# Two chained cross-attention layers on one core: an attention transfer issued in the first step, ScalarE's half of some norms a step later, output weights' sums in step 24, one copy of e by VectorE, the last pair in two stores

## The chip, the cores and the metric

The kernel runs on one core of one Trainium2 chip. The core has TensorE (PE in the profile, its weight loads PEld), VectorE (DVE), ScalarE (ACT), GpSimd (POOL) and SyncE (SP), and 16 DMA engines that the queues of SP, ScalarE and GpSimd feed. The metric is the device time of one execution in microseconds: the median over several executions. All data is float32.

## The reference

Inputs are `x` and a context, both [32, 256, 256]: 32 batches of 256 tokens of width 256. The first layer is an attention with 16 heads between `x` and the context, of which only batch 0 is used and added to every batch. The second layer is, for every batch, a cross-attention from the sum (normalised) to the context (normalised), a hidden layer of width 4 with GELU, a self-attention on its normalised output, and two skip connections.

```python
att = attention(tgt @ Wq.T, memory @ Wk.T, memory @ Wv.T)   # 16 heads of 16
x = tgt + att[0]                                            # batch 0's, added to all 32

norm_X   = layernorm(ctx, norm1_w, norm1_b)
norm_F_L = layernorm(x, norm2_w, norm2_b)
attended = softmax(norm_F_L @ norm_X.T / 16) @ norm_X
h = gelu(attended @ fc1_w.T + fc1_b)                        # width 4
cross = h @ fc2_w.T + fc2_b
norm_cross = layernorm(cross, norm3_w, norm3_b)
self_att = softmax(norm_cross @ norm_cross.T / 16) @ norm_cross
out = norm_F_L + gamma2 * (cross + gamma1 * self_att)
```

## The kernel before

A batch's 256 tokens lie two to a partition, so one batch of x is a [128, 2, 256] piece of the tile `x_all` (batch n, an even and an odd half), and likewise for the context in the tiles `cq` (four batches to a tile, four tiles). Everything stays in SBUF; each batch is loaded once and stored once.

**Stage 1 (to about 34 us)** is the first layer on batch 0. Its result is the tile `att`. From there on `att` has to be added to all 32 batches. Batches 0 to 3 are added by VectorE (`add_first`, and line 844 for batch 2). The others are added by transfers that `add_attention(lo, hi)` (L750) issues on GpSimd's queue, four batches and 1 MB to a transfer, with the DMA engines adding to what `x_all` holds.

**Stage 2** is `first_step(s)` (L869), called for s = 0 to 31 and, for what trails behind, 32 to 34. Step s does the scores and the exponentials of batch s. Around them it works ahead and behind: it turns e of batch s-2 (`cross_turned`), takes the statistics (VectorE) of x and of the context of batches some steps ahead, forms their means and factors (`moments_...`, on GpSimd, with one slow power instruction, L227), normalises (`norm_x`, `norm_c`), turns x of batch s+1 (`turn_x`) and the context of batch s+4 (`turn_c`). For a batch of x, `norm_x` (L326) gives the even half to GpSimd (L329) and the odd half to ScalarE (L331); ScalarE's instruction stands in that engine's queue between the copies of the turned x of the same step (L761, into `nfT`) and the exponentials (L792). Every four steps a group of four batches goes through `values`, `cross_values` and `cross_weighted`, and the lists `between` (inside the step, ahead of its scores) and `beside` (behind the step) add the work of the hidden layer and the first scores of the self-attention (`early_scores`, `early_weights`), step by step. The self-attention is done on vectors of 5 or 6 numbers, with small Gram products on GpSimd (`times_gram`, L1010).

The engines run their instructions in the order in which this code emits them, each engine its own queue; semaphores hold an instruction until what it needs is there. PSUM has two banks each for the tags `tp` (turned x, context, and smaller pieces), `et` (turned e), and `sm` and `s` in stage 2, so a transpose also waits until the copy out of the bank it is given is done.

`output_gammas`, `output_bias` and `output_rows` (L645 to L658) form the rows of the output weights on VectorE, six instructions on 5 partitions, and copy them with eight small transfers on SP's queue into `w_out`, which the last stage multiplies with.

**Stage 3 (from about 175 us)** is the rest of the self-attention and the output, in an order written out by hand as a string of words (L1244); `o12@s1` is the output product of pair 12 (batches 24 and 25), `add12` the sum of it with `x_all` on VectorE (`output`, L1211), followed by the pair's store on SP's queue. The stores are 512 KB each, 16 in all.

```python
        if s in (2, QB):
            add_attention((s // 2 + 2) * QB, (s // 2 + 3) * QB)
        elif b == 0 and 1 < q < NQ - 3:
            add_attention((q + 3) * QB, (q + 4) * QB)

        late_turn = s in (27, 29, 31)
        if 0 <= s - 2 < B and not late_turn:
            cross_turned(s - 2)
```

(QB is 4, B is 32; q and b are s // 4 and s % 4.)

Of the kernel before, what the change touches and what calls it, by code (L numbers as in the profile page):

```python
# [22 lines left out]
QB = 4  # L23
# [4 lines left out]
def tile_xattn_seq(  # L28
# [33 lines left out]
    nc = tc.nc  # L62
    B = x.shape[0]
# [16 lines left out]
    def bank(tag, name):  # L80
        return ps.tile([P, NC, D], F32, tag=tag, name=name)


    x_all = const.tile([P, B, NC, D], F32)
# [3 lines left out]
    def by_tokens(src):  # L88
        return src.rearrange("b (p t) d -> p b t d", t=NC)

    def load_c(q, first=0, queue=nc.sync):
        if q not in cq_of:
            cq_of[q] = ld.tile([P, QB, NC, D], F32, tag="cq", name=f"cq_{q}")
        n = 1 if first else QB
        lo = q * QB + (1 if first == 2 else 0)
        hi = q * QB + (1 if first == 1 else QB)
        queue.dma_start(cq_of[q][:, lo - q * QB : hi - q * QB], by_tokens(mem[lo:hi]))

    def load_x(lo, hi):
        nc.sync.dma_start(x_all[:, lo:hi], by_tokens(x[lo:hi]))  # L100
# [96 lines left out]
    def turned(src, tag, name, psum=None):  # L197

        pt = psum(f"pt_{name}") if psum else bank(tag, f"pt_{name}")
        for dc in range(NC):  # L200
            for t in range(NC):
                nc.tensor.transpose(  # L202
                    pt[:, dc, t * P : (t + 1) * P], src[:, t, dc * P : (dc + 1) * P], ident
                )
        return pt
# [39 lines left out]
    st_of, mc_of, mx_of = {}, {}, {}  # L245
# [7 lines left out]
    def stats_c(n):  # L253
        q, b = n // QB, n % QB
        statistics(st_tile(q - 1)[:, 0, b], cq_of[q][:, b])

    def stats_x(n):
        q, b = n // QB, n % QB
        statistics(st_tile(q)[:, 1, b], x_all[:, n])
# [16 lines left out]
    def moments_x(q, lo, hi):  # L276
        rn = moments(flat(st_of[q][:, 1, lo:hi]), (hi - lo) * NC, f"x{q}_{lo}")
        for b in range(lo, hi):
            mx_of[q * QB + b] = *rn, (b - lo) * NC
# [44 lines left out]
            )  # L324

    def norm_x(n, even=nc.gpsimd):  # L326
        rs, nmr, i = mx_of.pop(n)
        row = x_all[:, n, 0, :]
        even.tensor_scalar(row, row, rs[:, i, :], nmr[:, i, :], ALU.mult, ALU.add)  # L329
        row = x_all[:, n, 1, :]  # L330
        nc.scalar.activation(  # L331
            row, row, AF.Identity, bias=nmr[:, i + 1, :], scale=rs[:, i + 1, :]
        )


    nxT_of, nfT_of, col_of, eT_of, e_of = {}, {}, {}, {}, {}
# [324 lines left out]
    on_scalar = nc.scalar.copy  # L661

    by_vector = nc.vector.tensor_copy
# [86 lines left out]
    def add_attention(lo, hi):  # L750
        nc.gpsimd.dma_start(
            x_all[:, lo:hi],
            att.unsqueeze(1).to_broadcast([P, hi - lo, NC, D]),
            accum_op=ALU.add,
        )
# [38 lines left out]

        return softmax

    def cross_turned(n):
        q, b = n // QB, n % QB
        if b == 0:
            eT_of[q] = wk.tile([P, QB, NC, D], F32, tag="eTq", name=f"eTq_{q}", bufs=2)  # L800
        nc.scalar.copy(eT_of[q][:, b], turned(e_of.pop(n), "et", f"e_{n}"))  # L801

    def values(q):

# [22 lines left out]
    def add_first(n):  # L827
        nc.vector.tensor_add(x_all[:, n], x_all[:, n], att)
        stats_x(n)
# [39 lines left out]
    def first_step(s, between=()):  # L869
        q, b = s // QB, s % QB  # L870
        if b == 0 and 2 <= q and q + 4 < NQ:
            load_c(q + 4)
            if q == 2:
                load_x((NQ - 2) * QB, B)
        if s in (2, QB):
            add_attention((s // 2 + 2) * QB, (s // 2 + 3) * QB)
        elif b == 0 and 1 < q < NQ - 3:
            add_attention((q + 3) * QB, (q + 4) * QB)

# [3 lines that stand above are left out]
        if 2 <= s < 2 * QB:  # L883
            for n in (2 * s, 2 * s + 1):
                stats_x(n)
            if s < QB:
                ends = first_moments(2 * s, 2 * s + 2)
        if QB <= s and s + 3 * QB < B:
            stats_c(s + 3 * QB)
        if s >= 2 * QB and s + 2 * QB < B:  # L890
            stats_x(s + 2 * QB)
        if b == QB - 1 and 4 <= q + 2 < NQ:
            if q + 3 < NQ:
                moments_both(q + 2)
            else:
                moments_x(q + 2, 0, QB)
        if QB < s < B - 1:
            turn_x(s + 1)
        for n in {9: (12,), 10: (13, 14), 11: (15,)}.get(s, ()):
            norm_x(n)  # L900
        if 3 * QB <= s < B - 2 * QB:
            norm_x(s + QB)
        elif B - 2 * QB < s <= B - QB:
            norm_x(s + QB - 1)
        if s + QB < B and s >= QB:
            turn_c(s + QB, on_scalar if s < QB + 2 else by_vector)
        for n in {7: (13,), 8: (14, 15), 9: (16, 17), 10: (18,)}.get(s, ()):
            norm_c(n)
        if 2 * QB + 2 < s < B - 2 * QB:
            norm_c(s + 2 * QB)  # L910
        for n, at in enumerate(scaled_at):
            if s == at:
                scale_skip(n)
        if 2 * QB <= s < 2 * QB + len(zeroed):
            nc.gpsimd.memset(*zeroed[s - 2 * QB])
        if b == 2 and 1 < q < NQ:
            values_turned(q)
        if b == 1 and 1 < q < NQ:
            values(q)
        if b == 2 and 0 < q <= NQ:  # L920
            cross_values(q - 1)
        if b == 3 and 0 < q <= NQ:
            cross_weighted(q - 1)
        for f, *args in between:
            f(*args)
        if s < B:
            softmax = cross_scores(s)
            if s <= QB:
                turn_x(s + 1)
            if s == 0:  # L930
                turn_c(6, nc.scalar.copy)
            softmax()
        if late_turn:
            cross_turned(s - 2)
        if 1 <= s <= QB:
            stats_c(s + 3 * QB - 1)
        if s == 0:
            first_ends.pop()()
            add_first(3)
            first_ends.append(first_moments(3, QB))  # L940
            odd_normed(7)
        elif s == 1:
            first_ends.pop()()
            odd_normed(8)
            even_normed(8, 9)
        elif s == 2:
            ends()
            turn_c(7)
            load_c(5)
            odd_normed(9)  # L950
            even_normed(10)
        elif s == 3:
            ends()
            values(1)
            even_normed(11)
        elif s == QB:
            values_turned(1)
        if s in (QB, QB + 1):
            odd_normed(s + 6)
        if s == QB:  # L960
            moments_x(2, 0, 2)
        elif s == QB + 1:
            norm_x(2 * QB)
            moments_x(2, 2, QB)
        elif s == QB + 2:
            norm_x(2 * QB + 1)
            moments_c(3)
            norm_x(2 * QB + 2)
            norm_c(3 * QB)
        elif s == QB + 3:  # L970
            norm_x(2 * QB + 3)
        elif s == 2 * QB:
            moments_both(3)
# [146 lines left out]
    def divide(g, pa):  # L1120
        rd = small.tile([P, TQ, 1], F32, tag="rd2", name=f"rd2_{g}")
        nc.vector.reciprocal(rd, pa[:, :, NM : NM + 1])
        nc.vector.tensor_mul(
            v_flat[:, g * TQ : (g + 1) * TQ, NM : 2 * NM],
            pa[:, :, 0:NM],
            rd.to_broadcast([P, TQ, NM]),
        )
# [25 lines left out]
    def activate(lo):  # L1153
# [1 line left out]

    between = {
        20: [(hide, 0, 4)],
        24: [(output_gammas,)],
        25: [(output_bias,)],
        27: [(output_rows,)],  # L1160
        28: [(turn_t, 0, by_vector)],
        29: [(turn_u, 2, by_vector), (early_weights, 0), (hide, 4, 6)],
        30: [(activate, 4), (third_a, 2), (turn_t, 1, by_vector)],
# [3 lines left out]
        20: [(activate, 0), (third_a, 0)],  # L1167
        21: [(third_b, 0), (third_a, 1)],
        22: [(third_c, 0), (third_b, 1)],
        24: [(third_d, 0)],  # L1170
        25: [(third_c, 1), (turn_u, 0, by_vector)],
        26: [(turn_u, 1, by_vector), (early_scores, 0), (third_d, 1)],
        28: [(early_scores, 1)],
# [37 lines left out]
    def output(p, pieces):  # L1211
        for lo, hi, po in pieces:
            xs = x_all[:, 2 * p + lo : 2 * p + hi]
            nc.vector.tensor_add(xs, po, xs)  # L1214
        nc.sync.dma_start(by_tokens(out[2 * p : 2 * p + 2]), x_all[:, 2 * p : 2 * p + 2])


    held = {}

# [35 lines left out]
    turn_t6 add8 scale27 sums7 tT6 add7 turn_v5 col7 scale28 o9@s1+k12@s0 vT5 k13@et  # L1255
    add9 exp12 scale29 turn_a7 exp13 o10@s0+o11@s1 scale30 a7 sums6 add10 scale31
    turn_v7 col6 add11 vT7 turn_a6 o15@s0+o14@et a6 turn_v6 add15 vT6 o12@s1 add14
    o13@s0 add12 add13
    """

    def turn_a(g):
# [15 lines left out]
    def pre(lo):  # L1277
# [9 lines left out]
        "max": lambda p: scores_max(p, held.pop(("q", p))),  # L1287
        "exp": lambda p: weights(p, held.pop(("k", p))),
        "add": lambda p: output(p, held.pop(("o", p))),
        "a": lambda g: divide(g, held.pop(("a", g))),  # L1290
        "sums": sums,
        "col": col,
# [69 lines left out]
```

## Time and profile before

| | |
|---|---|
| time, median of 3 | 227.26 us (227.24 to 228.19) |
| the profiled execution's own time | 228.16 us |
| its span in the profile | 226.4 us |
| TensorE, VectorE, ScalarE, GpSimd busy | 208.1, 169.8, 146.6, 175.3 us |
| bytes moved by DMA | 33.81 MB |
| ScalarE's waits for GpSimd's factors at L331 | 11.0 us in 4 waits |
| last sum of VectorE done | 221.42 us |

The span runs from the first to the last instruction of the program; the time has some 2 us around it. In the profile a row of the timeline has its start in us from the span's start, its length in us, the engine, the line of the kernel, the operation, the tiles written and read with buffer numbers left out, the shape, and in brackets for how long the engine stood idle before it and what ended that. A row of the chain has start, length, engine and line: it is the way back from the last instruction, each time to what released it. Since an engine's queue is strictly in order, an instruction that waits holds all those behind it on that engine.

### The profile page before, as it was taken

How to read it: one execution, taken by the hardware profiler on the slowest of the kernel's cores; microseconds unless marked ns; L12 is line 12 of the kernel's file. 1: busy time of each engine (PE TensorE's matmuls, PEld its weight loads, DVE VectorE, ACT ScalarE, POOL GpSimd, SP SyncE). 2: the span in 40 equal slices, each digit the busy share in tenths (PEclk: the TensorE clock that was granted, in tenths of full speed). 3: DMA queues.
4: the chain of work that ended last, by engine and by line, in shares of the span. 5: the costliest groups of instructions: out<-in, count | busy, mean ns of one | idle time of the engine just before them, and what ended most of it. 6: DMA issues, size and time to landing. Idle time of an engine off the chain costs nothing.

```text
span 226.4 us, 4951 instructions
## 1 busy us (share of the span) xinstructions
PE 208.1 (92%) x1797; PEld 152.6 (67%) x1797; DVE 169.8 (75%) x406; ACT 146.6 (65%) x301; POOL 175.3 (77%) x276
## 2 busy tenths in 40 slices
PE   7899988898999989999999999998998999999960
PEld 6666547576787859688798697685756566666640
DVE  2787989898988766768767578596546699978791
ACT  2454877698979359576868986448594684545510
POOL 6056588567889999999979989999229888999700
PEclk9999999999999999999999999999999999999996
DMA  6699998998976994082280000000000031542786
GB/s 210 214 310 375 389 386 225 179 263 246 208 145 244 305 195 185 0 147 43 48 142 0 1 3 0 0 3 5 5 1 0 3 126 62 210 164 92 278 308 254
DMA packets 18038, 33.81 MB, mean 149 GB/s; under 512 B 1175, under 2 KB 2142, under 8 KB 18014
## 3 DMA queue, kind: packets, MB, share of 16 engines
q1 hardware_dynamic: 12974, 24.33, 30.1%
q0 software_dynamic: 3696, 7.34, 18.6%
q10 hardware_dynamic: 1344, 1.84, 2.5%
q8 instruction: 14, 0.23, 0.4%
q14 instruction: 10, 0.08, 0.1%
HBM read 17.73 MB, written 8.39 MB: 115 GB/s over the span
## 4 chain that ended last, share of the span: by engine, by line
PE 45%; POOL 22%; DVE 14%; DMA 8%; ACT 5%; issue 3%; DVEq 1%; ACTq 0%; SPq 0%; POOLq 0%
PE sc L779 8%; POOL cq L307 6%; PE o L445 4%; DMA x_all<-att 4%; POOL rs_b L227 4%; PE k L445 4%; DVE st L211 4%; PE pu L357 4%; POOL x_all L329 3%; PE sc L445 2%; PE q L445 2%; DVE nm L789 2%; DMA wk_nat<-in_L_xattn_Wk_dram 2%; DMA fc_nat<-in_L_xattn_fc_w_dram 2%; POOL rs_x L227 2%
## 5 line engine op out<-in xcount | busy, mean ns | idle before, releaser
L779 PE MATMUL sc<-nxT,nfT 128*128 128x256 f32 x256 | 62.4, 386 | 0.7 <-ACT nfT L761 0.7
L779 PEld LDWEIGHTS sc<-nxT,nfT 128*128 128x128 f32 x256 | 45.7, 190 | 12.1 <-issue 5.3
L770 POOL TENSOR_TENSOR x_all<-x_all,w_bc 128x512 f32<-128x512 f32 x32 | 39.8, 1278 | 0.0
L792 ACT ACTIVATE e<-sc,nm 128x256 f32<-128x256 f32 x64 | 26.9, 474 | 19.2 <-DVE nm L789 19.0
L789 DVE TENSOR_REDUCE nm<-sc 128x2 f32<-128x512 f32 x32 | 22.0, 688 | 22.3 <-PE sc L779 10.7
L761 ACT ACTIVATE nfT<-pt_x,bq,wq 128x256 f32<-128x256 f32 x64 | 33.3, 583 | 1.6 <-PE pt_x L202 1.5
L211 DVE BATCH_NORM_STATS2 st<-x_all 128x6 f32<-128x256 f32 x64 | 23.2, 412 | 1.5 <-DMA x_all<-att 1.4
L202 PE MATMUL pt_x<-ident,x_all 128*128 128x128 f32 x132 | 20.4, 276 | 1.5 <-POOL x_all L329 1.3
L202 PE MATMUL pt_c<-ident,cq 128*128 128x128 f32 x132 | 19.7, 276 | 1.9 <-ACT nfT L761 1.4
L1214 DVE TENSOR_TENSOR x_all<-o,x_all 128x1024 f32<-128x1024 f32 (+1 forms) x20 | 19.3, 1005 | 2.9 <-PE o L445 2.4
L202 PE MATMUL pt_e<-ident,e 128*128 128x128 f32 x128 | 19.5, 275 | 1.3 <-ACT eTq L801 0.7
L211 DVE BATCH_NORM_STATS2 st<-cq 128x6 f32<-128x256 f32 x56 | 20.6, 412 | 0.0
L1209 ACT ACTIVATE eT<-k 128x512 f32<-128x512 f32 (+1 forms) x19 | 14.3, 798 | 9.1 <-PE k L445 7.8
L307 POOL TENSOR_SCALAR cq<-cq,rs_b,nmr_b 128x256 f32<-128x256 f32 x32 | 19.4, 679 | 0.0
L202 PEld LDWEIGHTS pt_e<-ident,e 128*128 128x128 f32 x128 | 15.4, 141 | 5.0 <-ACT e L792 1.6
L801 ACT COPY eTq<-pt_e 128x512 f32<-128x512 f32 x32 | 18.4, 588 | 0.3 <-PE pt_e L202 0.3
L202 PEld LDWEIGHTS pt_x<-ident,x_all 128*128 128x128 f32 x132 | 15.2, 141 | 4.6 <-POOL x_all L329 2.4
L202 PEld LDWEIGHTS pt_c<-ident,cq 128*128 128x128 f32 x132 | 15.0, 141 | 3.6 <-ACT nfT L761 2.4
L345 DVE COPY nxT<-pt_c 128x512 f32<-128x512 f32 x23 | 15.6, 677 | 2.4 <-PE pt_c L202 2.4
L331 ACT ACTIVATE x_all<-x_all,nmr_b,rs_b 128x256 f32<-128x256 f32 x16 | 9.8, 619 | 11.0 <-POOL nmr_b L236 11.0
L445 PE MATMUL o<-w_out,vt 32*128 32x256 f32 x128 | 13.3, 400 | 0.6 <-ACT vt L1088 0.5
L445 PE MATMUL k<-tt,ut 32*128 32x256 f32 x112 | 13.6, 397 | 0.0
(222 smaller groups left out, 435.6 us busy)
## 6 DMA issues: line engine op xcount, KB each, us to landing
out_dram<-x_all SPq DMA_DIRECT2D x16, 512.0 KB
x_all<-att POOLq DMA_DIRECT2D x7, 1024.0 KB, 9.8
cq<-in_ctx_dram SPq DMA_DIRECT2D x6, 1024.0 KB
x_all<-in_x_dram SPq DMA_DIRECT2D x4, 1024.0 KB
x_all<-in_x_dram SPq DMA_DIRECT2D x1, 2048.0 KB
x_all<-in_x_dram SPq DMA_DIRECT2D x1, 1792.0 KB
cq<-in_ctx_dram ACTq DMA_DIRECT2D x1, 1024.0 KB
cq<-in_ctx_dram SPq DMA_DIRECT2D x1, 768.0 KB
```

What stands on the lines that cost most here:

```text
L202: nc.tensor.transpose(pt[:, dc, t * P : (t + 1) * P], src[:, t, dc * P : (dc + 1) * P], ident)
L211: nc.vector.bn_stats(st[:, t, :], src[:, t, :])
L307: nc.gpsimd.tensor_scalar(row, row, rs[:, i + t, :], nmr[:, i + t, :], ALU.mult, ALU.add)
L345: copy(nxT_of[q][:, b], pt)
L445: nc.tensor.matmul(dst[i][:, t, :], lhs[r : r + SL, t * P : (t + 1) * P], rhs[r : r + SL, :], start=True, stop=True,)
L761: nc.scalar.activation(nfT_of[n][:, dc, :], px[:, dc, :], AF.Identity, bias=bq[:, dc : dc + 1], scale=wq2[:, dc : dc + 1],)
L770: nc.gpsimd.tensor_mul(x_all[:, n], x_all[:, n], w2_bc.unsqueeze(1).to_broadcast([P, NC, D]))
L779: nc.tensor.matmul(sc[:, qt, :], nfT[:, dc, qt * P : (qt + 1) * P], nxT[:, dc, :], start=(dc == 0), stop=(dc == NC - 1),)
L789: nc.vector.tensor_reduce(nm, sc, AX.X, ALU.max, negate=True)
L792: nc.scalar.activation(e[:, qt, :], sc[:, qt, :], AF.Exp, bias=nm[:, qt : qt + 1])
L801: nc.scalar.copy(eT_of[q][:, b], turned(e_of.pop(n), "et", f"e_{n}"))
L1214: nc.vector.tensor_add(xs, po, xs)
```

## The change

Five edits:

- The transfer that adds `att` to batches 12 to 15 is issued by GpSimd at the end of step 0, after batch 2's normalisation, not at the front of step 2.
- `norm_x` is taken apart into `even_x` (GpSimd) and `odd_x` (ScalarE). GpSimd's half stays where it was. ScalarE's half of batches 12, 16 and 20 is issued a step later (steps 10, 13 and 17), together with that of 13, 17 and 21; that of batch 14 moves from step 10 to step 11.
- `output_gammas` and `output_bias` stand behind step 23 (they were inside steps 24 and 25), `output_rows` with its eight transfers behind step 24 (it was inside step 27).
- The copy of the turned e of batch 29 out of PSUM, in step 31, is done by VectorE and no longer by ScalarE.
- The last pair (13) is summed and stored batch by batch: two sums of 128 x 512 and two stores of 256 KB, where one sum of 128 x 1024 and one store of 512 KB stood.

```diff
     def norm_x(n, even=nc.gpsimd):
-        rs, nmr, i = mx_of.pop(n)
+        even_x(n, even)
+        odd_x(n)
+
+    def even_x(n, even=nc.gpsimd):
+        rs, nmr, i = mx_of[n]
         row = x_all[:, n, 0, :]
         even.tensor_scalar(row, row, rs[:, i, :], nmr[:, i, :], ALU.mult, ALU.add)
+
+    def odd_x(n):
+        rs, nmr, i = mx_of.pop(n)
         row = x_all[:, n, 1, :]
         nc.scalar.activation(
             row, row, AF.Identity, bias=nmr[:, i + 1, :], scale=rs[:, i + 1, :]
...
-    def cross_turned(n):
+    def cross_turned(n, copy=nc.scalar.copy):
...
-        nc.scalar.copy(eT_of[q][:, b], turned(e_of.pop(n), "et", f"e_{n}"))
+        copy(eT_of[q][:, b], turned(e_of.pop(n), "et", f"e_{n}"))
...
-        if s in (2, QB):
-            add_attention((s // 2 + 2) * QB, (s // 2 + 3) * QB)
+        if s == QB:
+            add_attention(QB * QB, (QB + 1) * QB)
...
         for n in {9: (12,), 10: (13, 14), 11: (15,)}.get(s, ()):
-            norm_x(n)
+            even_x(n)
         if 3 * QB <= s < B - 2 * QB:
-            norm_x(s + QB)
-        elif B - 2 * QB < s <= B - QB:
+            even_x(s + QB)
+
+        for n in {10: (12, 13), 11: (14, 15), 12: (), 13: (16, 17), 16: (), 17: (20, 21)}.get(
+            s, (s + QB,) if 3 * QB <= s < B - 2 * QB else ()
+        ):
+            odd_x(n)
+        if B - 2 * QB < s <= B - QB:
             norm_x(s + QB - 1)
...
         if late_turn:
-            cross_turned(s - 2)
+            cross_turned(s - 2, by_vector if s == B - 1 else on_scalar)
...
         if s == 0:
             first_ends.pop()()
+            add_attention(3 * QB, 4 * QB)
             add_first(3)
...
     between = {
         20: [(hide, 0, 4)],
-        24: [(output_gammas,)],
-        25: [(output_bias,)],
-        27: [(output_rows,)],
...
     beside = {
...
-        24: [(third_d, 0)],
+        23: [(output_gammas,), (output_bias,)],
+        24: [(third_d, 0), (output_rows,)],
...
+    def output_each(p, pieces):
+
+        (_, _, po), = pieces
+        for n in range(2):
+            xs = x_all[:, 2 * p + n]
+            nc.vector.tensor_add(xs, po[:, n], xs)
+            nc.sync.dma_start(by_tokens(out[2 * p + n : 2 * p + n + 1]), x_all[:, 2 * p + n : 2 * p + n + 1])
...
-    o13@s0 add12 add13
+    o13@s0 add12 each13
...
         "add": lambda p: output(p, held.pop(("o", p))),
+        "each": lambda p: output_each(p, held.pop(("o", p))),
```

## The prediction

> **What bounds the kernel now.** I read the page's busy shares first, then the chain that ended last in order of time, then the waits, then each engine's timeline around the edited steps. A step is one batch of the middle stage (scores 0 begin at 40.25 us, scores 31 at 170.16); the last stage runs from 175 us.
>
> ```profile
> PE 208.1 (92%) x1797; PEld 152.6 (67%) x1797; DVE 169.8 (75%) x406; ACT 146.6 (65%) x301; POOL 175.3 (77%) x276
> PE 45%; POOL 22%; DVE 14%; DMA 8%; ACT 5%; issue 3%; DVEq 1%; ACTq 0%; SPq 0%; POOLq 0%
> ```
>
> TensorE is busy 92%, yet less than half of the chain lies on it. The chain, piece by piece:
>
> ```profile
> 50.19 0.55 POOL x_all L751
> 50.99 1.50 POOL rs_x L227
> ...
> 109.96 9.85 DMA x_all<-att
> 119.90 0.75 DVE st L211 x2
> ...
> 153.04 0.61 DVE nm L789
> 154.05 0.47 ACT e L792
> 154.52 0.48 ACT eTq L801
> 155.05 1.63 PE sc L445 x16
> ...
> 173.82 0.48 ACT eTq L801
> 174.35 0.66 PE pt_e L202 x4
> ```
>
> First line: the issue that the change moves stands itself on the chain. From about 64 to 110 us the chain runs through POOL to the issue of the last attention sum, that transfer lands 9.85 us later, and VectorE's statistics of batch 28 wait for it. The lines at 153 to 155 and 174 are two more waits that the change touches. The waits view names the longest one it means to remove, and one that is short now:
>
> ```profile
> ACT x_all L331 <- POOL nmr_b L236: 11.0, 4, 5.1
> DVE st L211 <- DMA x_all<-att: 1.4, 2, 0.9
> ```
>
> The windows (length, then PE, PEld, DVE, ACT, POOL busy, clock, DMA share, GB/s) of POOL's stretch and of the tail:
>
> ```profile
> 58.00:117.00 59.00, 56.95 (x427) 45.63 (x426) 44.57 (x115) 42.73 (x96) 55.77 (x107) 1.00 0.66 153
> 219.00:222.00 3.00, 0.15 (x2) 0.00 (x0) 2.43 (x3) 0.00 (x0) 0.00 (x0) 1.00 1.01 378
> ```
>
> POOL has 3 us free in 59, so it paces that stretch; at the end the DMA engines are full and TensorE is done. Rows of the timelines that price the edits:
>
> ```profile
> 52.52 0.16 DVE L236 TENSOR_TENSOR nmr_x<-nmean_x,rs_x 128x4 f32<-128x4 f32 x1 [0.51 <-POOL rs_x L227]
> 135.72 1.24 DVE L646 TENSOR_TENSOR g1r<-g1r,g2r 5x256 f32<-5x256 f32 x1
> 139.58 0.40 DVE L650 TENSOR_TENSOR tail<-tail,g1r 5x256 f32<-5x256 f32 x1
> 151.76 0.95 DVE L654 TENSOR_TENSOR g2r<-g2r,bias 5x256 f32<-5x256 f32 x1
> ```
>
> **The change, part by part.** All against the profiled execution: span 226.4 us, its own time 228.16; the median shown is 227.26, so the shift found on the span is taken off 227.26.
>
> *The transfer of batches 12 to 15.* Its issue leaves POOL at 50.13 (1.28 us; the next instruction began 0.86 later and ran 1.49 where its kind takes 1.01). There POOL's power for batches 4 and 5 could start when VectorE's input is done (50.68) and end near 51.75 instead of 52.48. VectorE is without gaps before and after, so it gains its one gap, 0.51, and everything that hangs on it (batch 4's normalisation, TensorE's 0.69 wait at 53.40, POOL's start at 56.97, which waits for VectorE) moves with it: -0.5. At the new place POOL has finished batch 2 at about 45.8 and next waits for VectorE until 46.85; 1.28 ends at 47.1, so it delays that power by 0.1, and its user runs at 48.29 anyway: 0. The transfer joins one still under way (batches 8 to 11, issued 37.76, landed 51.55); if the queue is served in order it starts then and lands near 58, where it landed at 62.22 for a use at 63.03. Had it stayed, that 0.8 would have shrunk. Other end: it halves the rate of batches 8 to 11, which then land near 54.5; their use is at 57.12, so still 0. SP is not passed.
>
> *ScalarE's half a step later.* Taken away: ScalarE stands from 76.6 to 81.79 (5.14), 3.00 before 93.23, 2.15 before 108.27. TensorE lost of this 1.64 (scores 10 to 11 take 5.00 against 3.36 in the like step 14 to 15), 0.91 (scores 13 to 14, 5.36 against 4.45) and about 0.1. But I price it at nothing. What is late next is POOL's chain: batches 24 to 27 are summed by a transfer issued at 95.66, landed 104.96; VectorE's statistics wait for it at 104.98 (0.48), then VectorE empties the transposed context 20, and TensorE's transpose of batch 18 needs that bank (it ran at 106.47, 0.09 late already). The same again at 119.81. POOL's work up to both issues is the same, so TensorE arrives up to 2 us early and waits. Bounds: 0 to -0.2 (the slack of the transpose of batch 22, 121.48 against 121.24). Taken 0. No cost: the new waits of ScalarE, in steps 10, 13 and 17, end at the same POOL values and ScalarE has under 3.2 us of work in them.
>
> *Output weights.* Two effects. First, the four instructions of the gammas and the bias now stand on VectorE behind the maxima of step 23 (done 134.46) and ahead of the copy of transposed context 28 (135.12 to 135.75). Alone they take 4 x 0.40; but L646 took 1.24 and ended 0.27 after POOL's Gram product (135.35 to 136.69), L654 0.95 and ended 0.28 after a POOL product. L650 took 0.40 beside a POOL power. So a product of two SBUF operands waits for a POOL product, not for a power. In the new place: first 134.46 to 134.86 (power), second to 135.2, third behind POOL's 0.34 to 135.7, fourth behind the Gram product (pushed back to 135.7) to 137.3; then the copy to 137.9. The transpose of batch 26 is given the PSUM bank that this copy empties, and ran at 137.08: +0.85. Bounds: 0 (no blocking, copy ends 136.5) to +1.45 (the power blocks too).
> The Trainium skill, page "SBUF — State Buffer", section "Who interferes with whom", says that a VectorE instruction with two SBUF inputs and a GpSimd one that reads SBUF exclude each other for the whole instruction. By the rows of L646 and L654 the trace agrees; L650 beside a power does not, and by the rule taken to the letter this term would be the +1.45 above.
>
> Second, the two products of step 27 (151.76 to 152.97, 1.21) leave the front of the maxima of scores 27, which are ready at 150.95. The maxima then start at 151.76, exponentials end at 153.2, the two bank copies at 153.75 and 154.25. TensorE comes free at 154.1 instead of waiting until 155.05 (0.87), and its 1.63 of early scores, half held by the second bank, becomes about 1.2: next transpose at 155.3 against 156.60. Bounds -0.87 and -1.3; taken -1.25, since nothing else it needs is later than 154.3. In step 24 the two products find room: VectorE's work between the maxima of 23 and those of 25 becomes 6.4 after 134.46, so 140.9, and these start at 141.15. The eight small transfers move on SP from 152.7 to about 140; behind them SP has only the first store, at 183.37: 0.
>
> *Copy of e, batch 29, by VectorE.* ScalarE did it after the exponentials (173.72); the transpose of batch 31 waited 0.67 for its bank. VectorE is free after the maxima at 172.9 and ends a 0.60 copy (its like copies are 0.59 to 0.69) at 173.5; the transpose starts at 173.7. VectorE's copy of u for group 3 and the division slip by 0.6, not needed before 175.3. The reduction at 177.50 waits for a POOL product ending 177.26, which does not move: later steps keep some 0.5. Bounds 0 to -0.67, taken -0.5.
>
> *Last pair in two stores.* The sum splits into 0.69 + 0.60 against 1.22, +0.1; SP issues once more (0.37). Stores issued from 218.06 are 4 x 524 KB, 5.5 us at 378 GB/s, from 219.2 to 224.78: the engines still hold 0.7 MB when the last is issued, so an earlier half waits in line. 0, with ends +0.3 (the wait of SP for one more landing) and -0.6 (half a store at the window's rate).
> The Trainium skill, "DMA: Bandwidth & Descriptors", section "Anatomy of one DMA", gives a transfer about 2 us plus its bytes over 436 GB/s; as an estimate by it, a last store of half the size ends 0.6 us earlier. The 1.01 share in the tail speaks against it.
>
> Sum: -0.5 + 0 + 0.85 - 1.25 - 0.5 + 0 = -1.4. The last stage is almost all TensorE on the chain, and POOL's last scaling ends 213.8 for a use at 216.74, so it passes the shift on: 227.26 - 1.4 = **225.9 us**.
>
> **The rivals.**
> (a) The gammas are not held (POOL starts its Gram product after them, or the transpose takes another bank): the +0.85 falls away, and some of the early copies' full gain comes: -2.3, 225.0. For it: the order against POOL turns on 0.1 us. Against: L646 and L654 both were held.
> (b) Held for long, by the power too, and step 28 gives its lower bound: -0.5 + 1.45 - 0.87 - 0.5 = -0.4, 226.8. For it: the moved block meets POOL at its densest. Against: L650.
> (c) ScalarE's freed 2.6 us count after all, if POOL's transfers land earlier than POOL's order says: -2.6 more, 223.3. Against: VectorE waited for both landings.
> (d) Slower: POOL holds the moved issue until batches 8 to 11 have landed (51.55). Then the power for batch 3 starts at 52.8 and not 47.0, the front of the stage loses some 5, less the other gains 0.9: 231. It decides as soon as the issue lasts past 48. Against: the issue at 37.76 took 1.31 with one transfer in flight until 43.76, the same number as now.
> (e) The transfer's place does nothing since VectorE's gap at 52 is filled by another wait: -0.9, 226.4.
>
> **How the numbers follow.** Forecast 0.46 (its own range 225.4 to 226.3), (a) 0.18, (b) 0.13, (c) 0.03, (d) 0.07, (e) 0.13. A measurement of this kernel tells about 0.5%, 1.1 us, from no change: 226.1 and 228.4 are the bounds. Of the forecast's 0.46, 0.34 lies under 226.1; with (a) and (c) faster is 0.55; the rest of the forecast, (b) and (e) make 0.38 the same; (d) is slower, 0.07. Range: from (a) with the tail's better end to (b) with its worse: 224.7 to 227.1; outside are (d), (c) and some ends.
>
> **What would show it.** POOL's issue at about 45.8, rs_x of batches 4 and 5 without it in front and the 0.51 gone; ScalarE's wait for nmr_b down from 11.0 to under 4, while VectorE's wait for x_all<-att grows from 1.4 to 3 or more; one of the four small products of step 23 over 1 us and TensorE waiting for nxT there; no 0.87 and 0.67 waits for eTq; DMA share near 1 to the end. The prediction is wrong if the landing waits of VectorE do not grow, or if POOL has idle time between 60 and 110.

## The result, and the profile after

The changed kernel took 226.29 us (median, 225.64 to 226.50), beside 227.70 us (227.24 to 228.29) of the kernel before taken alongside: ratio 0.994, 95% interval 0.993 to 0.996. Run once more beside other runs of before it gave 226.26 us and 0.9945 [0.9925, 0.9966]. The forecast was 225.9, which is 1.4 us off the time before (227.26); the medians taken side by side differ by 1.41, and 226.29 lies in the range of 224.7 to 227.1. The sum came out, but one of its terms did not, and it is the one that taught most.

The profiled execution took 226.24 us with a span of 224.5; the whole of it is 1.9 shorter than the profiled execution of before. Busy shares and the chain by engine (from the page of the changed kernel) hardly moved:

```profile
PE 207.7 (93%) x1797; PEld 152.7 (68%) x1797; DVE 170.2 (76%) x408; ACT 146.5 (65%) x300; POOL 174.3 (78%) x276
PE 43%; POOL 23%; DVE 16%; DMA 8%; ACT 4%; issue 3%; DVEq 0%; ACTq 0%; SPq 0%; POOLq 0%
```

The chain of the changed kernel in order of time (start, length, engine, tile and line):

```profile
109.31 9.24 DMA x_all<-att
118.64 0.75 DVE st L211 x2
...
130.96 2.94 POOL r L1061
133.97 0.61 POOL u_sl L1064
134.64 1.40 POOL w_k L1023
136.04 0.49 POOL vgv L1043
137.06 0.63 PE pt_x L202 x4
...
154.19 1.29 PE sc L452 x13
...
171.84 0.44 PE pt_e L202 x4
172.50 0.73 PE pt_e L202 x4
```

The transfer of the last attention sum and VectorE's statistics behind it still carry the chain; the piece from 131 to 137 is new; at 154 and 172 TensorE runs on where it waited before (0.87 and 0.67). The two waits, from the waits view:

```profile
ACT x_all L338 <- POOL nmr_b L236: 3.2, 4, 1.3
DVE st L211 <- DMA x_all<-att: 2.5, 2, 1.6
```

ScalarE's wait for POOL's factors fell from 11.0 to 3.2. Most of what it saves there it now stands elsewhere: its wait for VectorE's maxima (`ACT e <- DVE nm`) rose from 19.0 to 25.8. VectorE's wait for the landing rose from 1.4 to 2.5, and TensorE now waits behind it, since VectorE's copy out of the bank (`nxT`) comes after those statistics:

```profile
118.64 0.75 DVE L211 BATCH_NORM_STATS2 st<-x_all 128x6 f32<-128x256 f32 x2 [1.62 <-DMA x_all<-att]
119.31 0.67 DVE L352 COPY nxT<-pt_c 128x512 f32<-128x512 f32 x1
120.13 0.63 PE L202 MATMUL pt_x<-ident,x_all 128*128 128x128 f32 x4 [0.42 <-DVE nxT L352]
```

The windows of POOL's stretch and of the tail (length, then busy PE, PEld, DVE, ACT, POOL, clock, DMA share, GB/s):

```profile
58.00:117.00 59.00, 57.78 (x435) 47.02 (x434) 45.30 (x116) 44.36 (x98) 56.53 (x112) 1.00 0.64 152
219.00:222.00 3.00, 0.00 (x0) 0.00 (x0) 0.71 (x2) 0.00 (x0) 0.00 (x0) 0.59 1.02 381
```

POOL is as full as before (2.5 us free in 59), and so are the DMA engines between 219 and 222 us.

To see where the 1.84 us went, I took the start of each batch's scores on TensorE from the timelines and counted from the start of scores 0 (40.25 before, 40.18 after), which removes what stage 1 differs by:

| from scores 0 to | before | after | gained so far |
|---|---|---|---|
| scores 10 | 40.03 | 39.60 | 0.43 |
| scores 16 | 63.96 | 61.66 | 2.30 |
| scores 22 | 88.26 | 87.37 | 0.89 |
| scores 25 | 98.80 | 98.88 | -0.08 |
| scores 31 | 129.91 | 128.79 | 1.12 |
| first store issued | 143.12 | 141.42 | 1.70 |
| end of span | 186.12 | 184.28 | 1.84 |

The moved transfer gives the 0.43. The halves put TensorE 1.9 further ahead by scores 16, of which 1.4 is handed back by scores 22. The gammas and the bias cost 0.97 in step 24, the rows give back 1.20 in step 28, the copy gives 0.58.

### The profile page after: what moved, and what is told of

It is laid out like the page before. It is cut to its first block, busy times and chain, and to the rows that moved or that the text cites. A ratio compares the mean times of both kernels' runs of the same rounds, so it can differ in the third digit from the quotient of the medians.

```text
span 224.5 us, 4955 instructions
## 1 busy us (share of the span) xinstructions
PE 207.7 (93%) x1797; PEld 152.7 (68%) x1797; DVE 170.2 (76%) x408; ACT 146.5 (65%) x300; POOL 174.3 (78%) x276
## 3 DMA queue, kind: packets, MB, share of 16 engines
q10 hardware_dynamic: 1344, 1.84, 2.4%
## 4 chain that ended last, share of the span: by engine, by line
PE 43%; POOL 23%; DVE 16%; DMA 8%; ACT 4%; issue 3%; DVEq 0%; ACTq 0%; SPq 0%; POOLq 0%
PE sc L786 7%; POOL cq L307 6%; DVE st L211 5%; PE o L452 4%; DMA x_all<-att 4%; POOL rs_b L227 4%; PE k L452 4%; PE pu L364 4%; PE q L452 2%; PE sc L452 2%; POOL x_all L333 2%; DMA wk_nat<-in_L_xattn_Wk_dram 2%; DVE nm L796 2%; DMA fc_nat<-in_L_xattn_fc_w_dram 2%; PE ph L364 2%
## 5 line engine op out<-in xcount | busy, mean ns | idle before, releaser
L799 ACT ACTIVATE e<-sc,nm 128x256 f32<-128x256 f32 x64 | 26.9, 472 | 26.1 <-DVE nm L796 25.8
L1225 DVE TENSOR_TENSOR x_all<-o,x_all 128x1024 f32<-128x1024 f32 (+1 forms) x19 | 18.1, 993 | 2.9 <-PE o L452 2.4
L808 ACT COPY eTq<-pt_e 128x512 f32<-128x512 f32 x31 | 17.9, 584 | 0.2 <-PE pt_e L202 0.2
L1207 DVE TENSOR_REDUCE t_sl<-q 128x4 f32<-128x1024 f32 (+1 forms) x12 | 12.3, 1041 | 0.3 <-PE q L452 0.2
```

The source lines that it names most:

```text
L799: nc.scalar.activation(e[:, qt, :], sc[:, qt, :], AF.Exp, bias=nm[:, qt : qt + 1])
```

## The experiments

All ratios below are to the kernel before, run alongside, with 95% intervals; 0.2% is 0.5 us.

### The transfer alone

```diff
-        if s in (2, QB):
-            add_attention((s // 2 + 2) * QB, (s // 2 + 3) * QB)
+        if s == QB:
+            add_attention(QB * QB, (QB + 1) * QB)
...
             first_ends.pop()()
+            add_attention(3 * QB, 4 * QB)
```

> The kernel before with nothing but the transfer for batches 12 to 15 issued at the end of step 0. Theory of the prediction: VectorE loses its 0.51 us gap at 52, the whole POOL stretch to 110 starts that much earlier, and both landings that VectorE waits for move with it: -0.5 us, ratio 0.998. Rival 1: another wait fills the gap, 0. Rival 2: part of the change's gain is that the two late transfers land sooner after their issue (7.96 and 9.24 us in the changed kernel against 9.30 and 9.85 before): if that comes from the moved transfer, it shows here as -1.0 or more, with landings near 8 and 9.2 us; if it is chance, the landings of these runs scatter between 8 and 10 us without order.

Measured: 227.28 us, 0.9978 [0.9959, 0.9998]. Counted from scores 0, scores 10 come at 39.59 instead of 40.03, and the last attention transfer is issued at 69.13 (69.71 in the profile before, 69.50 and 69.52 in two other kernels with the transfer at its old place). So the issue in step 2 cost 0.4 us, on POOL as on TensorE. In the profile of this run it is then lost: that transfer took 10.10 us to land instead of 9.85, and scores 22 stand at 88.17, 0.09 ahead. Rival 2 is out: the last two transfers landed 9.26 and 10.10 us after their issue, not near 8 and 9.2, so the shorter times of the changed kernel (7.96 and 9.24) do not come from the moved transfer.

### ScalarE's halves alone

```diff
         for n in {9: (12,), 10: (13, 14), 11: (15,)}.get(s, ()):
-            norm_x(n)
+            even_x(n)
         if 3 * QB <= s < B - 2 * QB:
-            norm_x(s + QB)
...
+            even_x(s + QB)
+        for n in {10: (12, 13), 11: (14, 15), 12: (), 13: (16, 17), 16: (), 17: (20, 21)}.get(
+            s, (s + QB,) if 3 * QB <= s < B - 2 * QB else ()
+        ):
+            odd_x(n)
```

> The kernel before with nothing but ScalarE's half of batches 12, 16 and 20 a step later. Theory: ScalarE's wait for nmr_b falls from 11.0 us to under 4, TensorE reaches the scores of step 15 some 2 us earlier, and all of it is lost at the two landings for batches 24 to 27 and 28 to 31, where VectorE's wait grows from 1.4 to 3 us or more: 0 to -0.3 us. Rival: the freed time counts, -1.5 to -2.6 us (ratio 0.989 to 0.993).

Measured: 227.40 us, 0.9984 [0.9965, 1.0003]. ScalarE's wait at the odd half fell to 3.1 us, VectorE's for the landings rose to 3.3 in three waits; scores 16 came 1.93 earlier than before, scores 22 only 0.52. The gain is made and handed back, as in the whole change. The last two transfers landed 8.01 and 9.27 us after their issue, as in the change (7.96 and 9.24; 9.29 and 9.85 before): the moved halves alone bring the shorter landings with them.

### The output weights alone

```diff
-        24: [(output_gammas,)],
-        25: [(output_bias,)],
-        27: [(output_rows,)],
...
-        24: [(third_d, 0)],
+        23: [(output_gammas,), (output_bias,)],
+        24: [(third_d, 0), (output_rows,)],
```

> The kernel before with nothing but the moved sums of the output weights. Theory: the four products of step 23 hold the copy of the turned context 28, TensorE waits 0.8 to 1.0 us in step 25; the two products gone from step 27 give 1.2 us back in step 28: -0.2 to -0.4 us in all, and in the profile the fourth product takes over 1 us. Rival (a): no hold, -1.2 us. Rival (b): the hold costs as much as the other end gives, 0 or slower.

Measured: 227.17 us, 0.9977 [0.9957, 0.9997]. Scores 24 to 25 took 5.10 us against 4.14 before (0.96 lost), scores 28 to 29 6.95 against 8.16 (1.21 gained). In the trace that is a net 0.25; the medians say 0.5 with an uncertainty as large.

### The copy of e alone

```diff
-    def cross_turned(n):
+    def cross_turned(n, copy=nc.scalar.copy):
...
-        nc.scalar.copy(eT_of[q][:, b], turned(e_of.pop(n), "et", f"e_{n}"))
+        copy(eT_of[q][:, b], turned(e_of.pop(n), "et", f"e_{n}"))
...
-            cross_turned(s - 2)
+            cross_turned(s - 2, by_vector if s == B - 1 else on_scalar)
```

> The kernel before with nothing but the copy of e of batch 29 by VectorE. Theory: TensorE's 0.67 us wait before the transpose of batch 31 is gone, -0.5 us. Rival: VectorE's next copies (u of group 3, the division) and the reduction at 177.5 take it back within 5 us of the profile: 0 to -0.1 us.

Measured: 226.76 us, 0.996 [0.9946, 0.9975]. The wait of TensorE for that bank is gone, and from scores 31 to the first store it takes 12.64 us against 13.21, 0.57 less. The ratio is larger than that, and so is the span; its profile says why: with nothing changed up to step 29, the last attention transfer landed 8.48 us after its issue instead of 9.85, and scores 22 came 0.74 earlier. The four ratios add to -1.0% (each with 0.2) where the whole change has -0.6%: hardly more than their errors, which share the same runs of the kernel before, and landings that differ by a microsecond from kernel to kernel are part of the difference.

### The change without the moved halves

```diff
-            even_x(n)
+            norm_x(n)
...
-            even_x(s + QB)
+            norm_x(s + QB)
...
-            odd_x(n)
```

> The change with ScalarE's halves issued together with POOL's, as before. Theory 1 (POOL's transfers and their landing pace batches 10 to 28, ScalarE's waits lie in the slack): ScalarE's wait for nmr_b goes back from 3 to about 11 us, VectorE's wait for the landings falls from 2.5 to about 1.5, and the time is at most 0.4 us above the change's: 226.3 to 226.7, ratio to the kernel before 0.994 to 0.996. Theory 2 (ScalarE's freed time counts in full, rival c): 1.5 to 2.6 us above the change, 227.8 to 228.9, ratio 1.000 to 1.005.

Measured: 226.80 us, 0.9951 [0.9928, 0.9974]: 0.2 us above the change by the ratios and 0.5 by the medians (less than these intervals can tell; in the two profiles it is 0.9 from scores 0 to the end), and not the 1.5 to 2.6 of the theory in which ScalarE's time counts in full. Its waits:

```profile
ACT x_all L338 <- POOL nmr_b L236: 10.8, 4, 5.1
...
DVE st L211 <- DMA x_all<-att: 1.6, 2, 1.2
```

7.6 us more of waiting on ScalarE, and well under 1 us of time. The last issue on POOL is not touched by the halves at all: it comes 69.12 us after scores 0 here, 69.13 with them. What differs is the landing, 10.14 against 9.24, and with it scores 22, 88.19 against 87.37. All profiles with POOL unrelieved agree on this (last attention transfer and scores 22, in us from scores 0):

| kernel | halves moved | issued | issue to landing | landed | scores 22 | scores 22 after landing |
|---|---|---|---|---|---|---|
| before | no | 69.71 | 9.85 | 79.56 | 88.26 | 8.70 |
| transfer alone | no | 69.13 | 10.10 | 79.23 | 88.17 | 8.94 |
| weights alone | no | 69.52 | 9.95 | 79.46 | 88.40 | 8.94 |
| change without halves | no | 69.12 | 10.14 | 79.25 | 88.19 | 8.94 |
| copy alone | no | 69.50 | 8.48 | 77.98 | 87.52 | 9.54 |
| halves alone | yes | 69.49 | 9.27 | 78.76 | 87.74 | 8.98 |
| the change | yes | 69.13 | 9.24 | 78.37 | 87.37 | 9.00 |
| the change again | yes | 69.12 | 9.23 | 78.35 | 87.37 | 9.02 |
| weights moved on (below) | yes | 69.13 | 9.49 | 78.62 | 87.57 | 8.95 |
| one store (below) | yes | 69.14 | 9.32 | 78.46 | 87.40 | 8.94 |

In eight of the ten, whatever was edited, scores 22 come 8.94 to 9.02 after the landing: that transfer sets TensorE's place there. In the kernel before it is 0.24 less, and one row accounts for it: VectorE's product `pre` behind the statistics took 0.29 us there, where it began 0.04 ahead of POOL's normalisation, and 0.53 in the eight. Where the transfer landed earliest (copy alone) the landing no longer held TensorE: VectorE did not wait for it, and scores 16 to 22 took 23.71 us, as they do in the three kernels with POOL relieved below.

### The output weights moved on

```diff
+        25: [(output_gammas,), (output_bias,)],
+        26: [(output_rows,)],
...
-        23: [(output_gammas,), (output_bias,)],
-        24: [(third_d, 0), (output_rows,)],
+        24: [(third_d, 0)],
```

The first two lines are in the dictionary `between`, so the sums stand inside steps 25 and 26.

> The change with the gammas' and the bias's sums in the middle of step 25 and the rows' products in the middle of step 26, so that none of the three stands in front of the copy of transposed context 28 in step 23 nor of the maxima of step 27. Theory 1 (the products are held by POOL's Gram product in front of that copy, and that is the 0.97 that TensorE loses in step 24): the products take 0.40 to 1.3 us at the new place, TensorE goes from scores 24 to scores 25 in 4.1 to 4.3 us instead of 5.1, and the time is 0.8 to 1.0 us below the change's: about 225.4, ratio 0.990. Theory 2 (the moved products delay VectorE's maxima of steps 25 to 27 as much): scores 25 come earlier but scores 29 do not, ratio 0.994 as the change.

Measured: 225.23 us, 0.9891 [0.9861, 0.9920], 1.1 us below the change by the medians; from scores 0 to the end the two profiles differ by 0.6: the last transfer took 0.25 longer to land here, and 0.2 stays in step 25 (below). The loss in the change can be read off two engines. VectorE's timeline of the changed kernel (start, length, line, operation, shape):

```profile
133.51 0.40 DVE L653 TENSOR_TENSOR g1r<-g1r,g2r 5x256 f32<-5x256 f32 x1
133.95 0.41 DVE L654 TENSOR_TENSOR g2r<-g2r,m 5x256 f32<-5x256 f32 x1
134.29 0.55 DVE L657 TENSOR_TENSOR tail<-tail,g1r 5x256 f32<-5x256 f32 x1
134.87 1.44 DVE L658 TENSOR_TENSOR g2r<-g2r,tail 5x256 f32<-5x256 f32 x1
136.24 0.67 DVE L352 COPY nxT<-pt_c 128x512 f32<-128x512 f32 x1
```

and POOL's, with TensorE's next transpose, in the same stretch:

```profile
130.96 2.93 POOL L1061 TENSOR_TENSOR r<-ve,neg_half 128x16 f32<-128x16 f32 x1
133.97 0.60 POOL L1064 TENSOR_TENSOR u_sl<-v_sl,r 128x80 f32<-128x80 f32 x1
134.64 1.40 POOL L1023 TENSOR_TENSOR w_k<-u_sl,gram_k 128x576 f32<-128x576 f32 x1
...
137.06 0.63 PE L202 MATMUL pt_x<-ident,x_all 128*128 128x128 f32 x4 [0.78 <-POOL sq_x L224]
```

The fourth product lasts until POOL's Gram product w_k is over, the copy comes behind it, and the transpose starts 0.15 after the copy's end (136.91). The name in the bracket, sq_x, is an operation that ran at 136.83 and that this transpose does not read; that the bank was what it waited for shows in the moved kernel, where its VectorE rows of step 25 are

```profile
138.91 0.40 DVE L653 TENSOR_TENSOR g1r<-g1r,g2r 5x256 f32<-5x256 f32 x1
139.34 0.41 DVE L654 TENSOR_TENSOR g2r<-g2r,m 5x256 f32<-5x256 f32 x1
139.69 0.41 DVE L657 TENSOR_TENSOR tail<-tail,g1r 5x256 f32<-5x256 f32 x1
140.13 0.67 DVE L658 TENSOR_TENSOR g2r<-g2r,tail 5x256 f32<-5x256 f32 x1
```

and scores 24 to 25 take 4.14 us again. Scores 25 to 26 take 5.57 against 5.39, and scores 28 to 29 the same 6.96: 0.8 of the 0.97 stay.

### POOL relieved

Of step 8's to 13's work POOL loses six memsets of 128x1024, 0.89 us each, to VectorE.

```diff
-            nc.gpsimd.memset(*zeroed[s - 2 * QB])
+            (nc.vector if s < 14 else nc.gpsimd).memset(*zeroed[s - 2 * QB])
```

> The change with six memsets of 128x1024 (0.89 us each in steps 8 to 13) on VectorE in place of POOL: POOL has 5.3 us less to do before it issues the sums of batches 20 to 31. Theory 1 (POOL's stretch to those issues and their landings swallow most of what the halves free on ScalarE): both transfers are issued 3 to 5 us earlier, VectorE's wait for x_all<-att falls from 2.5 to under 0.5 us, and TensorE keeps the 2.0 to 2.4 us that it is ahead at scores 16 through scores 22 instead of 1.0: 0.9 to 1.4 us below the change, 224.9 to 225.4, ratio 0.988 to 0.990. Theory 2 (something else, VectorE with 5 us more of its own work or ScalarE, paces these steps): no gain over the change or a loss of up to 2 us, ratio 0.994 to 1.003.

Measured: 223.44 us, 0.9815 [0.9783, 0.9846], 2.8 us below the change, twice what the theory gave it. The issues on POOL's timeline of the changed kernel

```profile
95.06 1.27 POOL L758 DMA_DIRECT2D x_all<-att  x1
109.31 1.26 POOL L758 DMA_DIRECT2D x_all<-att  x1
```

became, with POOL relieved,

```profile
91.09 1.27 POOL L758 DMA_DIRECT2D x_all<-att  x1
104.95 1.27 POOL L758 DMA_DIRECT2D x_all<-att  x1
```

VectorE's wait for x_all<-att is no longer in the waits view, and ScalarE's wait at the odd half shrank with it:

```profile
ACT x_all L338 <- POOL nmr_b L236: 0.6, 1, 0.6
```

The window that POOL paced now belongs to TensorE (same columns as above, kernel with POOL relieved):

```profile
58.00:117.00 59.00, 58.39 (x441) 48.40 (x441) 51.26 (x125) 45.46 (x101) 52.71 (x105) 1.00 0.65 149
```

0.6 us free on TensorE, 6.3 on POOL, and VectorE takes the 6 us without holding TensorE; POOL itself now waits 3.8 us for VectorE's statistics (`POOL df_b <- DVE st`), which it did not in the change. Scores 22 come at 84.65, 11.00 us after the landing where it was 9.00, so the landing no longer sets them: TensorE is 3.0 us ahead of the kernel before at scores 16 and 3.6 at scores 22. The first theory had counted only what the change handed back after scores 16 (1.4); the 0.7 that come on top by scores 16 are waits in steps 11 and 13 that were POOL's too (scores 11 to 12 took 3.29 in the change and 3.04 now, 13 to 14 4.88 and 4.46), and the 0.6 after it are steps 16 and 21 (4.26 and 5.06 in the kernel before, 4.13 and 4.59 now), where the kernel before had waited for landings as well.

### POOL relieved, without the moved halves

The two diffs above together: memsets on VectorE, `norm_x` in one piece.

> The change with the six memsets on VectorE, and ScalarE's halves issued with POOL's as before. Theory 1 (with POOL relieved TensorE itself paces steps 10 to 23, so that what ScalarE's waits cost TensorE is felt): 1.0 to 2.5 us above the kernel that has both (1.64 and 0.91 were lost in the kernel before; the lower end since POOL's values come earlier now too), 224.4 to 226.0, ratio 0.986 to 0.993. Theory 2 (the halves are worth no more than beside the loaded POOL, 0.5): at most 223.9, ratio 0.984 or less.

Measured: 224.76 us, 0.9873 [0.9854, 0.9893], 1.3 us above the kernel with both (0.6% with an uncertainty of 0.4). In the profiles scores 22 come at 85.35 against 84.65, 0.7 later; the rest of the difference in span, 1.0, lies ahead of scores 0 (40.82 against 39.80), where the two kernels are the same. The median lies in the first theory's range (1.0 to 2.5 above), but it gets there only with that difference ahead of scores 0: the halves are worth 0.7 in the steps that they touch, and at most some 1.3. The one row of TensorE's timeline between 79 and 107 us that still shows a wait:

```profile
83.73 0.66 PE L202 MATMUL pt_c<-ident,cq 128*128 128x128 f32 x4 [0.41 <-ACT nfT L768]
```

The losses of before (1.64 in step 10, 0.91 in step 13) were for the most part the memsets' doing. Against the change without the halves, from which this kernel differs by the memsets alone, scores 10 to 11 take 4.05 us and not 4.94, scores 13 to 14 4.45 and not 5.34, and ScalarE's wait is 6.6 us and not 10.8: POOL's values come earlier, and only step 10 still loses.

### One store

```diff
-    o13@s0 add12 each13
+    o13@s0 add12 add13
```

> The change with the last pair of outputs stored in one transfer, as before. Theory 1 (the DMA engines are full to the end, so that a half that is issued earlier waits in line): within 0.2 us of the change, ratio 0.993 to 0.996. Theory 2 (the last transfer's own length sets the end): 0.6 us above the change, ratio 0.997.

Measured: 226.62 us, 0.9955 [0.9934, 0.9975], against 0.9943 for the change: no difference that these intervals can tell. The profiles do tell: from the last sum's end to the last packet it is 3.31 us with one store, 3.22 and 3.26 with two (two profiles of the change). The half store gives 0.05 to 0.1 and its second sum costs 0.07.

### Both improvements together

The change with the memsets on VectorE and the output weights in steps 25 and 26.

> The change with the six memsets on VectorE and the products of the output weights in steps 25 and 26. Theory 1 (two losses in different steps, one in 16 to 22 and one in 24): both gains add, 1.0 us below the kernel with the memsets alone, 222.4, ratio 0.977. Theory 2 (the moved products meet VectorE's or POOL's other work now that all runs earlier): no gain over 223.4, ratio 0.981 or more.

Measured: 222.65 us, 0.9784 [0.9763, 0.9804], the fastest of all: 2.2% below the kernel before and 0.8 below the kernel with the memsets alone. Scores 24 to 25 take 4.14 us, scores 22 stand at 84.67. The two losses lay in different steps and both are won.

## Why the prediction was right, step by step

**The transfer, -0.5: right in place, 0.4 in size.** POOL issued it at 45.71, and VectorE's 0.51 in front of nmr_x is gone. POOL's timeline and VectorE's row in the changed kernel:

```profile
45.71 1.32 POOL L758 DMA_DIRECT2D x_all<-att  x1
46.95 0.84 POOL L227 TENSOR_TENSOR rs_x<-ve_x,neg_half 128x2 f32<-128x2 f32 x1
```

```profile
52.05 0.16 DVE L236 TENSOR_TENSOR nmr_x<-nmean_x,rs_x 128x4 f32<-128x4 f32 x1
```

The power behind it starts at 46.95, as forecast, so rival (d), in which the issue is held until 51.55, did not happen; nmr_x has no idle time in front of it any more, where it had 0.51. Rival (e), that another wait fills the gap, is out too: TensorE's scores 4 came 0.40 earlier and stayed so to scores 10. The transfer landed at 58.86, where I had estimated 58, and the one ahead of it on the queue 13.89 us after its issue, as before (13.79): the queue served them in order, and did not halve the rate of the first.

**ScalarE's halves, 0: the mechanism right, the size wrong.** The step said that POOL's issues and landings pace steps 16 to 22, so that TensorE would arrive early and wait. It did: 2.30 ahead at scores 16, 0.89 at scores 22, and the change without the halves is only 0.2 to 0.5 slower. POOL has 2.1 us free between 60 and 110 us, as before (2.2). What failed is the assumption behind the 0, that the landing follows POOL's issue by a fixed time (rival (c) names the other case). The issue did stay (69.12 without the halves and 69.13 with them), but in the profile of the change the transfer landed 9.24 us after it, and 9.85 before. These 0.6 cover the 0.46 that scores 22 gained beyond the 0.43 of the first edit. They also go with VectorE's wait for the landings growing to 2.5 only, where I had written 3 or more. The shorter landings belong to the moved halves, not to chance alone, since all five kernels with them and with POOL unrelieved have them (table above); why is argued at the end and not shown. Rival (c), 2.6 more, is refuted in its size by the change without the halves, though its condition, transfers that land earlier, came true by 0.6; freed time that counts once POOL is out of the way was worth 0.7 to 1.3 even with POOL relieved.

**Gammas and bias, +0.85: right, 0.97.** The order against POOL was not quite the forecast one: the power ended at 133.89, the third product took 0.55 beside a 0.60 product, the fourth 1.44. A VectorE product stood through POOL's Gram product and not through its power (133.51, 0.40 us, beside the power until 133.89). That decides between the sum's value and the +1.45 of rival (b). The Trainium skill, page "SBUF — State Buffer", section "Who interferes with whom", has the two exclude each other as soon as GpSimd's instruction reads SBUF, which a power does too; the rows of L658 and w_k agree with it, the row of L653 beside the power does not. Rival (a), the gammas not held, is out; moving them away made 0.8 us by scores 25 and 1.1 by the medians, about its price of 0.9.

**Rows, -1.25: right, -1.20 to -1.21,** in the change and alone. TensorE's early scores took 1.36 without a wait where they took 1.63 behind 0.87.

**The copy of e, -0.5: -0.57 alone, -0.58 in the change.** It is the better end of the range but for 0.1.

**The last pair, 0: right.** The engines moved 378 to 382 GB/s between 219 and 222 us in either form. The estimate of 0.6 worked out from the formula in "DMA: Bandwidth & Descriptors" of the Trainium skill, section "Anatomy of one DMA", is not borne out: 0.05 to 0.1 was seen. The page states that formula for transfers issued by GpSimd; these stores are issued on SP's queue, with the engines full.

The terms as measured, -0.43 - 0.46 + 0.97 - 1.20 - 0.58 - 0.14 (the tail), make the -1.84 of the two profiles; the forecast had -1.4. That the medians differ by exactly 1.4 (interval 0.9 to 1.7) is therefore partly luck: the two profiled executions are 0.5 further apart than the medians, and one term of -0.46 was missing. The range had a slip in its lower end: rival (a)'s 225.0 with the tail's better end, -0.6, is 224.4 and not 224.7; the measured 226.29 lies inside either way.

## What to carry to other kernels

A wait that is taken off one engine is worth only the slack of the next late thing; look for that (here an issue at the end of a full engine's queue and its landing) and shorten its queue first: six memsets on the wrong engine cost twice what the five edits won. Before instructions are moved into a gap, look at what the other engine that they exclude is doing there and at which copy stands behind them. A transfer's time from issue to landing is no constant to 1 us; a sum that hangs on one needs that spread as a bound.

## What the runs showed of the hardware

**Late landings went with an instruction load.** The last two attention transfers move 1 MB each at the same rate in all runs (95% of their packets were done 5.55 to 5.61 us after the first began), yet landed 7.96 to 10.14 us after their issue. The traces hold a load of 16 KB, one packet on a queue marked "instruction", near both, and the time to landing goes with where it falls. DMA queues of the kernel before between 117.5 and 119.0 us (packets, MB, share of 16 engines):

```profile
q8 instruction: 1, 0.02, 4.0%
q0 software_dynamic: 3, 0.00, 1.0%
```

Here the load ran from 117.78 to 118.74, and the transfer's last packet ended at 118.74 too; 95% of its packets had been done at 117.35. It landed at 119.81. In the kernel with the copy alone, between 117.6 and 119.0 us:

```profile
q8 instruction: 1, 0.02, 4.0%
q0 software_dynamic: 1, 0.00, 0.1%
```

the load ran from 117.69 to 118.58, just behind the transfer's last large packets (117.71), and it landed at 118.25. Over all thirteen profiles: the last transfer took 9.23 to 10.14 us in the nine in which the load fell before the transfer's last packets, and 8.45 to 8.60 in the four in which it began within 0.03 us of their end. For the transfer before it, 7.96 to 8.20 in the five with the load at its first packets, 8.70 and 8.93 in the two with it in the first half, 9.26 to 9.49 in the four with it in the second half, and 8.47 and 8.65 in the two with it at the very end. In the ten kernels with POOL unrelieved the load came 6.83 to 7.27 us after the last issue where the halves were moved (landing after 9.23 to 9.49), and 7.82 to 8.10 where not (9.85 to 10.14, and 8.48 where it just missed the end). In all ten the load began 1.5 to 2.0 us after scores 19, and those came 6.3 to 6.4 us after the issue where the halves were not moved and 5.0 to 5.3 where they were: so it came at a place in the program, and the halves brought that place closer to the issue. That would explain the shorter landings. It is a coincidence seen thirteen times over, not an experiment: no run moved the load alone, and which engine's instructions it brings stays open.

**Six memsets on VectorE cost TensorE nothing there.** A memset of 128x1024 took 0.91 us on VectorE and 0.89 on POOL (its piece of the chain; the rows of POOL's timeline, which overlap, show 0.95 to 1.33); with six of them more, ScalarE's wait for VectorE's maxima, its longest, went from 25.8 to 26.0 us.
